# Order of the first loads, and the targets of routed rows, in a fused decoder layer

## The chip, the cores and the metric

The kernel runs on one core of one Trainium2 chip. The metric is the device time of one execution in microseconds (us). A core has TensorE (PE in the profile; its weight loads are PEld), VectorE (DVE), ScalarE (ACT), GpSimd (POOL) and SyncE (SP). Each engine works through its own queue of instructions in order. A DMA is issued by the queue of one engine, here SP or POOL, and moved by 16 DMA engines.

## The reference

A decoder layer in float32 on x of [4, 1024, 256], with a context of [4, 154, 256] and distances of [4, 1024, 154]:

```python
# self part: 16 heads of 16, queries modulated, beside a 4-head attention of the same tokens,
# and a 4-head attention over their mixture
mod = sigmoid(x @ cg_W + cg_b + (cons_vec @ am_W + am_b))
scores = (q @ k.T) / sqrt(16) * mod
ctx = 0.3 * softmax(scores) @ v + 0.7 * mha(x, x, ca)
ctx = 0.85 * ctx + 0.15 * mha(ctx, ctx, mc)
x = layernorm(x + ctx @ Wo + bo)
# cross part: 16 heads, bias from the distances
scores = (x @ Wq.T + bq) * 0.25 @ (c @ Wk.T + bk).T - log(distances + 1e-9) * abs(scaling)
x = layernorm(x + softmax(scores) @ (c @ Wv.T + bv) @ Wo.T + bo)
# feed-forward: the two best of 8 experts for each token, and a shared one
y = sum_e w[e] * (silu(x @ w_gate[e]) * (x @ w_up[e])) @ w_down[e]
out = layernorm(x + y + shared(x))
```

The meta weight 0.15 comes from (0.9 - 0.8) / 0.2 * 0.3.

## The kernel before

The work falls into a prologue, a loop over the four batches, the routing, the shared expert with the routed tiles, and a closing layernorm. Every tile is allocated from pools, and each engine's instructions stand in the order in which a scheduler at build time has put them; semaphores are placed where one engine's result is needed by another. DMAs of one kind (those of SP, those of POOL) take turns on eight completion semaphores, so that a DMA is issued only when the one eight places before it has landed.

**Prologue.** It loads the first batch (y0) and all attention weights and biases. `load_head_cols` loads a 256x256 weight through a staging tile, clears a tile of 128x1024 and copies each head's 16 columns into a field of 32 (L146, L148, on POOL). `load_head_bias` does the like with a bias in four small DMAs (L164, on POOL's queue); `load_cols` (L169) and `load_bcast` (L174) issue bias loads on POOL's queue too. `load_plain` (L138) issues weights on SP. The bias cgb of the modulation comes from four small matmuls (L212) on am and cons. The last loads of the prologue are the cross attention's weights and nds, the negated distance scaling. Then two DMAs on SP fill a DRAM tensor, `scratch` (9216 rows of 258 values): L260 writes zeros from `empty` into 256 of the 258 columns, L261 writes `rows` into the last two, of which the first is a row number of its own for each row, as the target of rows that no token fills.

**A batch's beginning**, the generator `begin(b)`. It transposes the tokens (L127, copied out by ACT at L130), fills v16 with ones on POOL (L761), projects mod, q and k for the first group of four heads (L288 with cgw, wq, wk; ACT at L392 and L408, POOL at L395, DVE at L401), and runs ahead with the first 12 steps of row maxima: a step is two row-tiled matmuls of q and k (L422) into a two-bank PSUM tile and one reduction on DVE (L429). Between the steps come the values v (L302 with wv, DVE at L310), after them the values of the second attention (L302 with cawin). Every eight steps the maxima are transposed (L343) and added to q (L346). For batches 1 to 3 this generator is spread over the cross part of the batch before; for batch 0 it is run through before the main loop of the batch. Ahead of it stand the loads of that batch's distances and context (L816, L818) on SP.

**The main loop** of a batch has 128 steps: maxima of step n+12, scores of step n (L460) into the three small PSUM banks and one more, exponentials on ACT (L471), and every fourth step the product with v (L480). At the steps 4, 8 and 12 of a group the next group is projected. The logarithm of the distances (L942 on ACT, with table loads of its own ahead of and behind it) and its product with nds (L943 on DVE) are written much later in the program, but have only the loads as inputs, and are put early in the queues by the scheduler.

**Routing and experts.** Gate probabilities give each token two experts, and from these a `place` in `scratch` for each of the two copies of a token. `tail` carries for each copy the row of `result` to which the expert's output goes (first of its two columns) and its weight. `send(b)` scatters tokens with their tails to `scratch` by indirect DMAs from POOL (L1127), beside the shared expert's matmuls (L1178, L1155). Then 72 tiles of 128 rows are fetched (L1198); `to` and `by` are taken from the two last columns (L1201, L1202 on POOL), the expert is applied (L1226, L1236, L1243, L1248), and the output is scattered to `result` by an indirect DMA over `to` (L1258).

Of the kernel before, what the change touches and what calls it, by code (L numbers as in the profile page):

```python
# [8 lines left out]
F32 = mybir.dt.float32  # L9
# [3 lines left out]
ALU = mybir.AluOpType  # L13
# [3 lines left out]
P = 128  # L17
B, S, H = 4, 1024, 256
# [4 lines left out]
NH, HD = 16, 16  # L23
# [10 lines left out]
RW = H + 2  # L34
TILES = 72
CAUSAL_W = 0.7
META_W = (0.9 - 0.8) / 0.2 * 0.3
# [3 lines left out]
def run(gen):  # L41
    for _ in gen:
        pass
# [3 lines left out]
def decoder_layer(ctx: ExitStack, tc: tile.TileContext, a, out):  # L47
    nc = tc.nc
# [25 lines left out]
    def load_y(b):  # L74
        ys.append(ypool.tile([P, NT, H], F32, tag="y", name=f"y{b}", bufs=2))
        nc.sync.dma_start(ys[b], xd[b])
# [12 lines left out]
    gw = const.tile([P, NC2, NE], F32, name="gw")  # L89
    dram = ctx.enter_context(tc.tile_pool(name="dram", bufs=1, space=bass.MemoryType.DRAM))  # L90

    scratch = dram.tile([TILES * P, RW], F32, name="scratch")
# [3 lines left out]
    def iota(dst, pattern, base, per_partition):  # L96
        nc.gpsimd.iota(
            dst,
            pattern=pattern,
            base=base,  # L100
            channel_multiplier=per_partition,
            allow_small_or_imprecise_dtypes=True,
        )
# [29 lines left out]
    with tc.tile_pool(name="wA", bufs=1) as wA, tc.tile_pool(name="work", bufs=2) as work:  # L133


        def load_plain(name, src, n):
            t = wA.tile([P, src.shape[0] // P, n], F32, tag=name, name=name)
            nc.sync.dma_start(t, src.rearrange("(c p) n -> p c n", p=P))  # L138
            return t

        def load_head_cols(name, src):

            st = work.tile([P, NC2, H], F32, tag="ex", name="stage", bufs=EXB)
            nc.sync.dma_start(st, src.rearrange("(c p) n -> p c n", p=P))
            t = wA.tile([P, NC2, NH, 32], F32, tag=name, name=name)
            nc.gpsimd.memset(t, 0.0)  # L146
            for c in range(NC2):
                nc.gpsimd.tensor_copy(  # L148
                    t[:, c, :, 0:HD], st[:, c, :].rearrange("p (h d) -> p h d", d=HD)
                )  # L150
            return t.rearrange("p c h w -> p c (h w)")

        def load_head_bias(name, src, extra):

            t = wA.tile([P, NG], F32, tag=name, name=name)
            if extra == 0.0:
                nc.vector.memset(t, 0.0)
            else:
                tmp = work.tile([P, NG], F32, tag="tmpb", name="tmpb")
                nc.vector.memset(tmp, extra)  # L160
                nc.vector.tensor_scalar(t, tmp, rowmx, None, ALU.mult)
            v = src.rearrange("(g j d) -> j d g", j=4, d=HD)
            for j in range(4):
                nc.gpsimd.dma_start(t[32 * j : 32 * j + HD, :], v[j])  # L164
            return t

        def load_cols(name, src):
            t = wA.tile([P, src.shape[0] // P], F32, tag=name, name=name)
            nc.gpsimd.dma_start(t, src.rearrange("(c p) -> p c", p=P))  # L169
            return t  # L170

        def load_bcast(name, src):
            t = wA.tile([P, H], F32, tag=name, name=name)
            nc.gpsimd.dma_start(t, src.unsqueeze(0).to_broadcast([P, H]))  # L174
            return t


# [7 lines left out]
            nc.gpsimd.memset(m, 0.0)  # L185
            mxcol.append(m)

        nc.sync.dma_start(gw, a["L0_ffn_gate_w"].rearrange("(c p) e -> p c e", p=P))
        wq = load_head_cols("wq", a["L0_attn_Wq"])
        bq = load_head_bias("bq", a["L0_attn_bq"], 0.0)  # L190

        cgs = work.tile([P, NC2, NH], F32, tag="cgs", name="cgs", bufs=1)
# [21 lines left out]
            )  # L214
        nc.vector.tensor_scalar(cgb, ps[:, 0:NG], 0.5, None, ALU.mult)

        wk = load_head_cols("wk", a["L0_attn_Wk"])
        bk = load_head_bias("bk", a["L0_attn_bk"], -1.0)
        wv = load_plain("wv", a["L0_attn_Wv"], H)
        bv = load_bcast("bv", a["L0_attn_bv"])  # L220
# [1 line left out]
        def load_mha(k, w_out):  # L222
            win = load_plain(k + "win", a[f"L0_attn_{k}_Win"], 3 * H)
            bin_ = a[f"L0_attn_{k}_bin"]
            mbq = load_cols(k + "bq", bin_[0:H])
            mbk = load_cols(k + "bk", bin_[H : 2 * H])
            mbv = load_bcast(k + "bv", bin_[2 * H : 3 * H])
            wout = load_plain(k + "wout", a[f"L0_attn_{k}_Wout"], H)
            bout = load_cols(k + "bout", a[f"L0_attn_{k}_bout"])
            nc.vector.tensor_scalar(bout, bout, w_out, None, ALU.mult)  # L230
            return win, mbq, mbk, mbv, wout, bout

        ca = load_mha("ca", CAUSAL_W)
        load_y(1)
        mc = load_mha("mc", META_W)
        wo = load_plain("wo", a["L0_attn_Wo"], H)
        bo = load_bcast("bo", a["L0_attn_bo"])
        xwq = load_head_cols("xwq", a["xWqT"])
        xbq = load_head_bias("xbq", a["L0_xattn_bq"], 0.0)
        xwk = load_head_cols("xwk", a["xWkT"])  # L240
        xbk = load_head_bias("xbk", a["L0_xattn_bk"], 0.0)
        xwv = load_plain("xwv", a["xWvT"], H)
        xbv = load_bcast("xbv", a["L0_xattn_bv"])
        xwo = load_plain("xwo", a["xWoT"], H)
        xbo = load_bcast("xbo", a["L0_xattn_bo"])

        nds = wA.tile([P, 1], F32, tag="nds", name="nds")
        nc.gpsimd.dma_start(nds, a["ds"].to_broadcast([P, 1]))
        nds2 = work.tile([P, 1], F32, tag="nds2", name="nds2", bufs=1)
        nc.vector.tensor_scalar(nds2, nds, -1.0, None, ALU.mult)  # L250
        nc.vector.tensor_tensor(nds, nds, nds2, ALU.min)


        empty = work.tile([P, H], F32, tag="avq", name="empty", bufs=3)
        nc.gpsimd.memset(empty, 0.0)
        rows = work.tile([P, TILES, 2], F32, tag="rb", name="rows", bufs=1)
        nc.gpsimd.memset(rows, 0.0)
        iota(rows[:, :, 0], [[P, TILES]], 2 * B * S, 1)
        sv = scratch.rearrange("(t p) w -> p t w", p=P)
        nc.sync.dma_start(sv[:, :, 0:H], empty.unsqueeze(1).to_broadcast([P, TILES, H]))  # L260
        nc.sync.dma_start(sv[:, :, H:RW], rows)  # L261


        def ex_tile(shape, name):
# [480 lines left out]
        def add_bias(y, bias):  # L745
            for t in range(NT):
                nc.gpsimd.tensor_tensor(y[:, t, :], y[:, t, :], bias, ALU.add)
# [5 lines left out]
        def begin(b):  # L753

            y = ys[b]
            xT = work.tile([P, NC2, S], F32, tag="xT", name="xT", bufs=1)
            for c in range(NC2):
                transpose_tokens(xT, y, c)
                yield
            v16 = work.tile([P, NT, VP], F32, tag="v16", name="v16", bufs=1)  # L760
            nc.gpsimd.memset(v16, 1.0)  # L761
            sa = Self(xT, v16, None)
            for step in (sa.project_mod, sa.project_q, sa.project_k):
                step(0)
                yield
            add_bias(y, bo)
            v64 = work.tile([P, NT, H], F32, tag="v64", name="v64", bufs=1)
            begun[b] = sa, xT, v64
            vals = values(xT, wv, 0, bv, v16, NH, HD, 1)
            for n in range(lead):  # L770
                sa.maxima(n)
                next(vals, None)
                sa.clock.step()
                yield
            yield from values(xT, ca[0], 2 * H, ca[3], v64, MH, MD, 0)

        def end(b, cx4):
# [28 lines left out]
            if b < B - 2:  # L806

                nc.sync.dma_start(kept[b].rearrange("(t p) d -> p t d", p=P), y)
                load_y(b + 2)

        behind = iter(())
        for b in range(B):
            y = ys[b]
# [3 lines left out]
            cn = work.tile([HK, 2, H], F32, tag="cn", name="cn", bufs=1)  # L817
            nc.sync.dma_start(cn, a["ctx_1024"][b].rearrange("(c p) d -> p c d", p=HK))  # L818

            if b == 0:  # L820
                run(begin(0))
            sa, xT, v64 = begun[b]
            sa.ctok = ctok = work.tile([P, NT, H], F32, tag="ctok", name="ctok", bufs=1)
            total = 16 * 8
# [177 lines left out]
    def rt(name, shape, dt=F32):  # L1002
        return xp.tile(shape, dt, tag=name, name=name)
# [9 lines left out]
    tail = rt("tail", [P, 2, NTT, 2])  # L1013
    ob = k1("ob", (P, 2, P))
    ones, before = ob[:, 0, :], ob[:, 1, :]
    iota(steps, [[P, NTT]], 0, 0)
    iota(tileno, [[1, TILES]], 0, 0)
    iota(tail[:, :, :, 0], [[B * S, 2], [P, NTT]], 0, 1)
    nc.gpsimd.memset(ones, 1.0)
    make_upper_triangular(nc, before, 1.0, diag=False)  # L1020

    red = rt("red", [P, NTT])
# [69 lines left out]
    for k in range(2):  # L1092
        mine = k1("mine")
        nc.vector.tensor_tensor(mine, hot[k], rank, ALU.mult)
        nc.vector.reduce_sum(red, mine, axis=AX.X)
        nc.vector.tensor_copy(place[:, k, :], red)


    owner = fw.tile([1, TILES, NE], F32, tag="hT", name="owner")
# [96 lines left out]
    def fetch(i):  # L1196
        xg = k1("xg", (P, RW))
        nc.sync.dma_start(xg, scratch[i * P : (i + 1) * P, :])  # L1198
        to = fw.tile([P, 1], U32, tag="to", name="to", bufs=5)
        by = fw.tile([P, 1], F32, tag="by", name="by", bufs=5)  # L1200
        nc.gpsimd.tensor_copy(to, xg[:, H : H + 1])  # L1201
        nc.gpsimd.tensor_copy(by, xg[:, H + 1 : H + 2])  # L1202
        ps = small()
        for c in range(NC2):
            nc.tensor.transpose(ps[:, c * P : (c + 1) * P], xg[:, c * P : (c + 1) * P], ident)
        xt = k1("xt", (P, NC2 * P))
        nc.scalar.copy(xt, ps[:, 0 : NC2 * P])
        xts[i] = xt, to, by
# [130 lines left out]
```

## Time and profile before

| | us |
|---|---|
| median of 3 runs | 3435.27 |
| lowest, highest | 3431.95, 3436.01 |
| the profiled execution's own time | 3433.82 |
| its span in the profile | 3432.0 |
| PE busy in the span | 3300.5 (96%) |
| DVE busy | 1725.3 (50%) |
| ACT busy | 1601.0 (47%) |
| POOL busy | 373.3 (11%) |

The profile is one execution. Times within it count from the start of the span. Its page shows the span in 40 slices of 85.8 us (a digit is a busy share in tenths; PEclk is the TensorE clock that was granted), the DMA queues, the chain of work that ended last, the costliest groups of instructions and the DMA issues. A line Lnnn is a line of the kernel. From the trace itself come the timeline, windows of chosen stretches, and the chain in order of time. An `x` behind a group counts instructions; a float32 matmul that is not a transpose is two of them.

### The profile page before, as it was taken

The numbers are of one execution on the slowest core, as the hardware profiler recorded it, in microseconds if no ns is written. First come the engines' busy times: TensorE is split into PE (matmuls) and PEld (weight loads), VectorE is DVE, ScalarE is ACT, GpSimd is POOL, SyncE is SP. The second block draws the span as 40 slices with busy tenths as digits, with TensorE's granted clock in tenths as the row PEclk, the third lists the DMA queues.
The fourth block names the chain that finished last, engine by engine and source line by source line (L and its number), as shares of the span: only waits on it lengthen the run. The fifth ranks groups of instructions, "written<-read, shape, count | busy, mean of one in ns | idle before, by whom it ended". The sixth has DMA issues, their size and how long they took to land.

```text
span 3432.0 us, 60936 instructions
## 1 busy us (share of the span) xinstructions
PE 3300.5 (96%) x25260; PEld 2085.6 (61%) x25260; DVE 1725.3 (50%) x3571; ACT 1601.0 (47%) x3130; POOL 373.3 (11%) x601
## 2 busy tenths in 40 slices
PE   7999999999999999999999999999999999999997
PEld 4555667565556675665566756555667665555554
DVE  3565555565655555656555556565556551122224
ACT  1555534375555453755554537555534731222223
POOL 4000000000000000000000000000000018222123
PEclk7999999999999999999999999999999999999999
DMA  9000000000000000000000000000000052111114
GB/s 204 1 2 1 1 1 1 3 21 14 1 1 1 1 1 3 21 13 2 1 1 1 1 3 9 1 2 1 1 1 1 1 203 82 47 42 44 44 44 157
DMA packets 75866, 84.13 MB, mean 25 GB/s; under 512 B 15136, under 2 KB 65928, under 8 KB 75592
## 3 DMA queue, kind: packets, MB, share of 16 engines
q1 hardware_dynamic: 68040, 61.53, 6.4%
q0 software_dynamic: 7552, 18.70, 1.6%
q8 instruction: 202, 3.31, 0.4%
q14 instruction: 72, 0.59, 0.1%
HBM read 46.52 MB, written 33.69 MB: 23 GB/s over the span
## 4 chain that ended last, share of the span: by engine, by line
PE 85%; DVE 9%; ACT 2%; issue 2%; POOL 1%; DMA 1%; SPq 0%; ACTq 0%; DVEq 0%; POOLq 0%
PE big L288 10%; PE big L422 8%; PE big L530 8%; PE one L566 7%; PE acc L584 7%; PE big L1226 7%; PE one L480 7%; DVE mxp L429 6%; PE one L460 4%; PE acc L1248 4%; PE one L697 3%; PE big L1178 3%; PE big L662 3%; PE one L302 2%; PE acc L716 2%
## 5 line engine op out<-in xcount | busy, mean ns | idle before, releaser
L429 DVE TENSOR_REDUCE mxp<-big 128x2 f32<-128x1024 f32 x512 | 610.3, 1218 | 305.5 <-PE acc L460 252.1
L422 PE MATMUL big<-k,q 31*128 31x512 f32 x2048 | 595.8, 644 | 30.2 <-DVE mxp L429 26.6
L471 ACT ACTIVATE ex<-one 128x512 f32<-128x512 f32 x696 | 391.3, 601 | 247.4 <-PE acc L460 182.9
L460 PE MATMUL one<-q,k 32*128 32x256 f32 x2784 | 501.9, 397 | 0.0
L269 DVE CUSTOM_DVE_ANT_0 prob<-big,zero_t 128x1024 f32<-128x1024 f32 x256 | 303.6, 1222 | 271.9 <-PE big L530 271.7
L460 PEld LDWEIGHTS one<-q,k 32*128 32x128 f32 x2784 | 326.8, 186 | 31.0 <-ACT ex L471 2.5
L549 ACT ACTIVATE prob<-prob,nmx 128x1024 f32<-128x1024 f32 x256 | 293.0, 1153 | 20.2 <-DVE nmx L269 19.7
L530 PE MATMUL big<-mk,mq 64*128 64x512 f32 x1024 | 284.4, 633 | 2.5 <-ACT ex L468 2.5
L422 PEld LDWEIGHTS big<-k,q 31*128 31x128 f32 x2048 | 180.1, 189 | 171.5 <-DVE mxp L429 93.6
L571 ACT COPY pt<-one 128x512 f32<-128x512 f32 x256 | 137.8, 588 | 311.7 <-PE one L566 311.7
L566 PEld LDWEIGHTS one<-ident,prob 128*128 128x128 f32 x2048 | 221.8, 142 | 98.1 <-issue 92.4
L1226 PE MATMUL big<-wall,xt 128*128 x576 | 272.5, 596 | 1.8 <-POOL by L1202 1.8
L460 PE MATMUL acc<-q,k 32*128 32x256 f32 x928 | 263.9, 404 | 0.0
L566 PE MATMUL one<-ident,prob 128*128 128x128 f32 x2048 | 257.6, 279 | 0.0
L480 PE MATMUL one<-ex,v 128*32 128x256 f32 x4096 | 248.4, 382 | 0.0
L1236 DVE TENSOR_TENSOR hidr<-big,slr 128x512 f32<-128x512 f32 x72 | 49.8, 691 | 332.7 <-ACT slr L1234 332.7
L682 ACT ACTIVATE xs<-xs,xmx 128x154 f32<-128x154 f32 x512 | 174.4, 414 | 69.6 <-DVE xmx L269 69.6
L480 PEld LDWEIGHTS one<-ex,v 128*32 128x32 f32 x4096 | 119.8, 110 | 122.1 <-ACT ex L471 35.8
L573 DVE COPY pt<-one 128x512 f32<-128x512 f32 x256 | 164.3, 683 | 10.9 <-PE one L566 10.9
L269 DVE CUSTOM_DVE_ANT_0 xs<-big,bias 128x154 f32<-128x154 f32 x512 | 132.0, 314 | 66.0 <-ACT avx L724 33.5
L530 PEld LDWEIGHTS big<-mk,mq 64*128 64x128 f32 x1024 | 99.6, 191 | 101.7 <-issue 79.4
L460 PEld LDWEIGHTS acc<-q,k 32*128 32x128 f32 x928 | 155.4, 186 | 0.0
(266 smaller groups left out, 4715.2 us busy)
## 6 DMA issues: line engine op xcount, KB each, us to landing
xg<-scratch SPq DMA_DIRECT2D x72, 129.0 KB, 2.0
scratch<-empty SPq DMA_DIRECT2D x1, 9216.0 KB
r<-result SPq DMA_DIRECT2D x8, 1024.0 KB, 11.2
y<-in_x_dram SPq DMA_DIRECT2D x4, 1024.0 KB, 5.3
wall<-in_L_ffn_w_gate_dram SPq DMA_DIRECT2D x8, 512.0 KB, 10.3
wall<-in_L_ffn_w_up_dram SPq DMA_DIRECT2D x8, 512.0 KB, 10.8
wall<-in_L_ffn_w_down_dram SPq DMA_DIRECT2D x8, 512.0 KB, 11.6
bias<-in_fside_BxSxS_dram SPq DMA_DIRECT2D x4, 616.0 KB, 4.5
```

Source lines behind the costliest of these rows:

```text
L269: nc.vector.tensor_tensor_reduce(out=out, in0=ps, in1=bias, scale=-1.0, scalar=3.0e38, op0=ALU.add, op1=ALU.min, accum_out=low,)
L288: nc.tensor.matmul(ps[:, tb, :], w[:, c, lo : lo + P], xT[:, c, tb * 512 : (tb + 1) * 512], start=(c == 0), stop=(c == NC2 - 1),)
L422: nc.tensor.matmul(ps[:, jj, :], st["q"][r : r + MR, tok : tok + P], st["k"][r : r + MR, kb * 512 : (kb + 1) * 512], start=True, stop=True,)
L429: nc.vector.reduce_max(mxp[:, t, kb, 2 * pair : 2 * pair + 2], ps, axis=AX.X)
L460: nc.tensor.matmul(scs[jj][:, i * QW : (i + 1) * QW], st["k"][r : r + MR + 1, kc * P : (kc + 1) * P], st["q"][r : r + MR + 1, part * QW : ...
L471: nc.scalar.activation(ex[:, jj, :], scs[jj], AF.Exp, scale=1.0 / HD**0.5)
L480: nc.tensor.matmul(av[32 * j : 32 * j + 32, 0:QW], self.v[:, kc, h * VW : h * VW + 32], exs[kc // 2, j // 2][:, j % 2, i : i + QW], start= ...
L530: nc.tensor.matmul(pss[i][:, kb, :], q[r : r + MD, t * P : (t + 1) * P], k[r : r + MD, kb * 512 : (kb + 1) * 512], start=True, stop=True,)
L549: nc.scalar.activation(p, p, AF.Exp, bias=nmx[:, i : i + 1], scale=-1.0, accum_out=sm[:, t % 4, i : i + 1],)
L566: nc.tensor.transpose(ps[:, kc * P : (kc + 1) * P], probs[u][i][:, at : at + P], ident)
L584: nc.tensor.matmul(av[64 * i : 64 * i + 64, (t % 4) * P : (t % 4 + 1) * P], v[:, kc, h * MD : (h + 1) * MD], flipped[u][i][:, kc, :], star ...
L1226: nc.tensor.matmul(ps[:, g, :], xt[:, c * P : (c + 1) * P], wall[:, bass.ds(off + (g * NC2 + c) * D, D)], start=(c == 0), stop=(c == NC2 - 1),
```

## The change

It has four parts. All small loads that stood on POOL's queue are issued by SP. The clearing and copying of wq and wk are done on DVE, those of xwq and xwk stay on POOL. The loads which the first batch's beginning does not need (the second batch's y, the gate, mc, Wo, the cross attention's weights and nds, the fill of scratch) stand in the program behind `run(begin(0))`, which is itself now ahead of the load of the distances. And the fill of scratch is one DMA of zeros over all 258 columns: `tail` holds a token's target less 8192 and the row that it is placed in, and a new tile, `own`, holds 8192 and the row's number (the row's own target) and is added when the tile is fetched, on DVE instead of POOL.

```diff
-        def load_head_cols(name, src):
+        def load_head_cols(name, src, eng):
...
-            nc.gpsimd.memset(t, 0.0)
+            eng.memset(t, 0.0)
             for c in range(NC2):
-                nc.gpsimd.tensor_copy(
+                eng.tensor_copy(
...
-                nc.gpsimd.dma_start(t[32 * j : 32 * j + HD, :], v[j])
+                nc.sync.dma_start(t[32 * j : 32 * j + HD, :], v[j])
...
-            nc.gpsimd.dma_start(t, src.rearrange("(c p) -> p c", p=P))
+            nc.sync.dma_start(t, src.rearrange("(c p) -> p c", p=P))
...
-            nc.gpsimd.dma_start(t, src.unsqueeze(0).to_broadcast([P, H]))
+            nc.sync.dma_start(t, src.unsqueeze(0).to_broadcast([P, H]))
...
-        wq = load_head_cols("wq", a["L0_attn_Wq"])
+        wq = load_head_cols("wq", a["L0_attn_Wq"], nc.vector)
...
         ca = load_mha("ca", CAUSAL_W)
-        load_y(1)
-        mc = load_mha("mc", META_W)
-        wo = load_plain("wo", a["L0_attn_Wo"], H)
         bo = load_bcast("bo", a["L0_attn_bo"])
-        xwq = load_head_cols("xwq", a["xWqT"])
...
-        empty = work.tile([P, H], F32, tag="avq", name="empty", bufs=3)
-        nc.gpsimd.memset(empty, 0.0)
-        rows = work.tile([P, TILES, 2], F32, tag="rb", name="rows", bufs=1)
-        nc.gpsimd.memset(rows, 0.0)
-        iota(rows[:, :, 0], [[P, TILES]], 2 * B * S, 1)
-        sv = scratch.rearrange("(t p) w -> p t w", p=P)
-        nc.sync.dma_start(sv[:, :, 0:H], empty.unsqueeze(1).to_broadcast([P, TILES, H]))
-        nc.sync.dma_start(sv[:, :, H:RW], rows)
...
+        run(begin(0))
...
+        load_y(1)
+        nc.sync.dma_start(gw, a["L0_ffn_gate_w"].rearrange("(c p) e -> p c e", p=P))
+        mc = load_mha("mc", META_W)
+        wo = load_plain("wo", a["L0_attn_Wo"], H)
+        xwq = load_head_cols("xwq", a["xWqT"], nc.gpsimd)
...
+        empty = work.tile([P, RW], F32, tag="rb", name="empty", bufs=1)
+        nc.gpsimd.memset(empty, 0.0)
+        nc.sync.dma_start(
+            scratch.rearrange("(t p) w -> p t w", p=P),
+            empty.unsqueeze(1).to_broadcast([P, TILES, RW]),
+        )
...
             nc.sync.dma_start(cn, a["ctx_1024"][b].rearrange("(c p) d -> p c d", p=HK))
-            if b == 0:
-                run(begin(0))
...
+    own = rt("own", [P, TILES])
+    iota(own, [[P, TILES]], 2 * B * S, 1)
...
         nc.vector.tensor_copy(place[:, k, :], red)
+        nc.vector.scalar_tensor_tensor(
+            tail[:, k, :, 0], tail[:, k, :, 0], -2.0 * B * S, red, ALU.add, ALU.subtract
+        )
...
-        nc.gpsimd.tensor_copy(to, xg[:, H : H + 1])
+        nc.vector.tensor_tensor(to, xg[:, H : H + 1], own[:, i : i + 1], ALU.add)
```

More of the change, by code (lines that the diff above doesn't have):

```diff
@@ L186, in decoder_layer @@
             mxcol.append(m)
-        nc.sync.dma_start(gw, a["L0_ffn_gate_w"].rearrange("(c p) e -> p c e", p=P))
-        wq = load_head_cols("wq", a["L0_attn_Wq"])
+        wq = load_head_cols("wq", a["L0_attn_Wq"], nc.vector)
         bq = load_head_bias("bq", a["L0_attn_bq"], 0.0)
@@ L215, in decoder_layer @@
         nc.vector.tensor_scalar(cgb, ps[:, 0:NG], 0.5, None, ALU.mult)
-        wk = load_head_cols("wk", a["L0_attn_Wk"])
+        wk = load_head_cols("wk", a["L0_attn_Wk"], nc.vector)
         bk = load_head_bias("bk", a["L0_attn_bk"], -1.0)
@@ L233, in decoder_layer @@
         ca = load_mha("ca", CAUSAL_W)
-        load_y(1)
-        mc = load_mha("mc", META_W)
-        wo = load_plain("wo", a["L0_attn_Wo"], H)
         bo = load_bcast("bo", a["L0_attn_bo"])
-        xwq = load_head_cols("xwq", a["xWqT"])
[L239 to L251, printed above, removed]
-        empty = work.tile([P, H], F32, tag="avq", name="empty", bufs=3)
-        nc.gpsimd.memset(empty, 0.0)
-        rows = work.tile([P, TILES, 2], F32, tag="rb", name="rows", bufs=1)
-        nc.gpsimd.memset(rows, 0.0)
-        iota(rows[:, :, 0], [[P, TILES]], 2 * B * S, 1)
-        sv = scratch.rearrange("(t p) w -> p t w", p=P)
-        nc.sync.dma_start(sv[:, :, 0:H], empty.unsqueeze(1).to_broadcast([P, TILES, H]))
-        nc.sync.dma_start(sv[:, :, H:RW], rows)
         def ex_tile(shape, name):
@@ L809, in end @@
                 load_y(b + 2)
+        run(begin(0))
[4 more added lines that the diff above has]
+        xwq = load_head_cols("xwq", a["xWqT"], nc.gpsimd)
+        xbq = load_head_bias("xbq", a["L0_xattn_bq"], 0.0)
+        xwk = load_head_cols("xwk", a["xWkT"], nc.gpsimd)
+        xbk = load_head_bias("xbk", a["L0_xattn_bk"], 0.0)
+        xwv = load_plain("xwv", a["xWvT"], H)
+        xbv = load_bcast("xbv", a["L0_xattn_bv"])
+        xwo = load_plain("xwo", a["xWoT"], H)
+        xbo = load_bcast("xbo", a["L0_xattn_bo"])
+        nds = wA.tile([P, 1], F32, tag="nds", name="nds")
+        nc.sync.dma_start(nds, a["ds"].to_broadcast([P, 1]))
+        nds2 = work.tile([P, 1], F32, tag="nds2", name="nds2", bufs=1)
+        nc.vector.tensor_scalar(nds2, nds, -1.0, None, ALU.mult)
+        nc.vector.tensor_tensor(nds, nds, nds2, ALU.min)
+        empty = work.tile([P, RW], F32, tag="rb", name="empty", bufs=1)
[4 more added lines that the diff above has]
+        )
         behind = iter(())
```

## The prediction

> **What bounds the kernel now.** I read the 40 slices first: TensorE is the bound nearly everywhere, except in the first slice.
>
> ```profile
> PE   7999999999999999999999999999999999999997
> PEclk7999999999999999999999999999999999999999
> DMA  9000000000000000000000000000000052111114
> ```
>
> Slice one (86 us) alone has a TensorE that is neither full nor at full clock, under a busy DMA. Next the table of windows for that slice (columns: window, length, PE, PEld, DVE, ACT, POOL busy, then granted clock, DMA share, GB/s):
>
> ```profile
> 24.00:27.00 3.00, 2.89 (x9) 1.33 (x7) 0.82 (x2) 0.00 (x0) 3.00 (x6) 1.00 1.05 273
> 27.00:32.00 5.00, 0.00 (x0) 0.00 (x0) 0.00 (x0) 3.61 (x3) 5.00 (x11) 0.99 0.30 58
> 32.00:36.00 4.00, 0.00 (x0) 0.00 (x0) 2.45 (x5) 0.00 (x0) 3.91 (x5) 0.50 0.96 307
> 36.00:69.00 33.00, 30.85 (x71) 11.73 (x71) 17.62 (x22) 0.00 (x0) 4.90 (x8) 0.50 1.22 252
> 69.00:72.00 3.00, 3.00 (x9) 2.46 (x8) 1.65 (x2) 0.00 (x0) 0.00 (x0) 0.50 1.86 6
> 72.00:76.00 4.00, 4.00 (x18) 3.44 (x18) 1.70 (x4) 0.00 (x0) 0.00 (x0) 0.90 0.88 5
> ```
>
> PE stands still from 27 to 36 while POOL is full; the clock halves at 32 and comes back only at 73. The loss is 9 us of waiting and some 41 us at half rate. What ends the wait is in the chain of work that ended last:
>
> ```profile
> 14.99 5.96 DMA cabq<-in_L_attn_ca_bin_dram
> ...
> 26.81 0.74 POOL xwk L148 x2
> 27.55 1.46 POOL xbk L164 x3
> ...
> 30.09 3.31 DMA nds<-in_ds_dram
> ...
> 35.63 0.42 DVE v L310
> 36.09 2.08 PE one L302 x4
> ```
>
> The chain runs through POOL's queue of small loads: v16's fill and mod (L761, L395) stand behind every bias load, and on DVE the first q and v (L401, L310) stand behind nds. Last, the timeline, for what the zeros of the scratch do to a DMA behind them on SP, and for when the main loop first needs ACT:
>
> ```profile
> 33.25 26.62 SPq L261 DMA_DIRECT2D scratch<-rows  x1
> 84.13 1.08 ACT L471 ACTIVATE ex<-one 128x512 f32<-128x512 f32 x2 [0.23 <-PE one L460]
> 87.55 0.38 PE L343 MATMUL one<-ident,mxcol 128*128 128x128 f32 x2
> 87.86 1.93 PE L480 MATMUL one<-ex,v 128*32 128x256 f32 x32
> ```
>
> The small DMA behind the zeros took 26.62 us to issue, and the issue table gives it 45.0 us to land.
>
> **What the Trainium skill says.** "DMA: Bandwidth & Descriptors", section "Queues, rings and completion order": each DMA engine takes one issuing engine's descriptors in ring order. The trace agrees: scratch<-rows landed only at 78, after zeros that moved until 67. The same page, "Issuing engines are not separate DMA queues": moving loads from POOL to SP saves only sequencer time; here that time is the point, as a POOL issue holds POOL for 0.5 to 0.75 us. "TensorE: Matmul & The Clock Gate", Part 1: TensorE falls to half rate after an idle window of about 3.4 us and recovers after a busy one. The fall agrees (idle from 26.9, half at 32); the recovery doesn't follow busy time alone: PE was 30.85 of 33 us busy at half rate, and it came back only after the first full window of 128x128 L302 matmuls (from 69). I count the narrow 31-row L422 as too little activity.
>
> **The change, part by part.**
>
> *POOL and the first q.* Ahead of v16's fill POOL loses four memsets (0.94 to 0.97), eight copies (0.37 each) and 29 DMA issues. The issues go to SP, the memsets and copies of wq and wk to DVE (idle then), those of xwq and xwk behind v16's fill on POOL, where the memsets end near 11 and the copies come after mod. DVE memsets and copies of these shapes are not in the trace before; bounded by POOL's 0.94 and DVE's own 0.42 for a 128x256 copy, all is over by 14 us, beside the transposes: nothing. In the new instruction streams nds, mcbout and the bias multiply stand behind the first maxima. So q and k follow the projections. am_b, cg_b and cons become 9th to 11th on SP; from the ninth DMA on each waits for the one eight before, the ninth for y (6.3 in the timeline), so cons lands near 9.3 and the four L212 matmuls come at 9.6 instead of 8.68; eleven transposes now stand before them instead of five, so cgw's projection starts near 13, as before. Three projections of 3.6 to 4.5 us end at 24.6, k on ACT 1.1 later: first L422 at 26 instead of 38.1.
>
> *The beginning's second half.* Before it took 38.1 to 78.0: alternating L422 and L302 groups of 2.01 and 2.00 us each at half clock. PE's gap is now under 2 us, so I take full clock: six steps at 2.15 (half of 4.01 and something for latencies; DVE needs 1.22+0.42), 12.9; two first steps at DVE's pace, 2.4; four reduces at 1.35 and a row fold, 6.1; 32 L302 at 0.24 (six took 1.46), 7.8. Sum 29.2: the main loop starts at 55, 23 us sooner.
>
> *What is late next: bias.* The streams put 48 DMAs ahead of it on SP: after 6.3 some 40 more at 0.6 us each (L138 issues took 0.4 to 1.3) bring the zeros at 31 (28 to 35), by chance as before (30.97). They moved at 290 to 300 GB/s from 32 to 67; with 1032-byte rows 34.5 us. bias (0.63 MB, 2 us, and 1 to landing) comes behind them: 31+34.5+3 = 68.5, between 63 and 75. cn follows, needed only in the cross stage. On ACT the Ln on bias (1.32) and two table loads (1.28 each) now stand after the first six exponentials, which end at 82.8-23 = 59.8. ACT then waits for bias. Behind it on ACT: the exponentials of steps 3 and 4, and on DVE the bias multiply, then reduces. PE runs on to L343 (64.5), where no small PSUM bank is free. ACT must do Ln, a load and three exponentials (1.32+1.28+1.7): L480 starts at 68.5+4.3 = 72.8 instead of 87.86, a gain of 15.1. The second table load was already paid before Ln. Note that the end of this stall doesn't depend on how fast the beginning gets there, up to 9 us: it takes back 8 of the 23.
>
> *Clock after the stall.* An idle of 8 us halves the clock again; L480 and L288 are dense, so one or two windows of 3.4 us at half rate: 1.7 to 3.4 lost, I take 2.6.
>
> *Routing.* Two DVE operations of 128x32 (0.18 to 0.29 for such shapes) and one iota (0.22) stand ahead of the sends; POOL's sends end at 2920.2, a us before PE's shared part, which hides them but for a tail: 0.3 at most. In the routed loop `to` moves from POOL (0.19) to DVE (0.15 by nds): DVE idles 4.5 us ahead of each L1236, and xg is loaded well ahead: nothing; if its DMA were late, PE's L1205 would wait for it anyway. rows, its iota and its 72 KB in 8-byte pieces go: nothing waited for them.
>
> **Sum.** -15.1 + 2.6 + 0.3 = -12.2 us on the profiled execution's 3433.82 (span 3432.0, 1.8 around it): 3421.6. That execution is 1.4 below the median 3435.27, so the median becomes 3423.
>
> **Rivals.**
> *bias is not held up* (the zeros' descriptors let it pass, or zeros issue early): gain 23 less 1.3 (Ln and loads 3.9 on an ACT with 2.6 idle there) and 0.3: 3414. Against: the 45.0 us of scratch<-rows. Chance 0.18.
> *SP becomes the bound*: 48 waits on eight lanes at nearly 0.8 us put the zeros at 38, bias at 75.5, L480 at 79.8: -8.1+2.6+0.3 = -5.2, 3430; with 36 or later up to no gain. For: issues that rose to 1.3 us near 13 us. Chance 0.14 for a gain under 7.
> *Slower*: one place, the zeros. If a 1032-byte row goes in two packets, or as a costlier write, bias comes later than 80.7 and the sum turns: that is from about 47 us of zeros, 81 ns a packet on 16 engines against 50 to 69 in the trace. With an 8-byte packet's mean of 31 added to 62: 53.6 us, bias at 88, L480 at 92: +4.4+2.6+0.3 = 3443. Against: reads of xg ran as whole 1032-byte packets. Chance 0.06.
> That the early loads do not get shorter at all is excluded by the streams; a clock that stays half in the beginning would end it at 66, still hidden by the stall.
>
> **How the numbers follow.** The likeliest case (bias at 63 to 75, gain 6 to 18) has 0.62, of which 0.60 is beyond 0.2% (6.9 us, about what a measurement of this kernel can tell from no change). With the first rival faster is 0.78; same 0.15; slower 0.07, the third rival and a stray clock. The range goes from 3410, the first rival's 3414 with one cold window less, to 3433, the second rival's near end, and leaves out some 0.12.
>
> **What would show it.** Right: PE without a hole between 25 and 36, first L422 near 26, clock 1.00 to about 60; then an ACT wait ahead of L942 released by the DMA of bias, DVE's L943 behind it, PE idle some 8 us before L343, half clock for 3 to 7 us after. Wrong: bias landing before 60 (first rival), zeros issued after 36 (second) or taking over 45 us (third), PE cold from 26 on, or a change in the routed loop's pace of 6 us a tile.

## The result and the profile after

| | before | after |
|---|---|---|
| median, us | 3435.64 (4 runs) | 3460.19 (4 runs) |
| lowest, highest | 3431.95, 3436.79 | 3458.6, 3467.14 |
| span of the profiled execution | 3432.0 | 3456.8 |

The ratio is 1.0081, 95% interval 1.0067 to 1.0095: **slower by 25 us**, where 12 us less were predicted, and above the top of the range. New line numbers stand 28 below the old ones in the attention (L394 was L422, L432 was L460, L443 was L471, L452 was L480, L315 was L343), and six above them in the expert part (L1184 was L1178, L1193 was L1187, L1169 was L1163, L1207 was L1201).

First the 40 slices of the changed kernel.

```profile
PE   7999999999999999999999999999999995999997
PEclk9999999999999999999999999999999997999999
```

The first slice got its clock back (9 instead of 7). But slice 34, from 2852 to 2938 us, has a PE at 5 tenths with a clock at 7, and there the kernel before had nines. Both traces hold the same 25260 matmuls, so the start of the k-th one can be compared, counted in each from the start of its span. The changed kernel is 9.2 us ahead at 100 us and 12.5 ahead at 2865. At 2940 it is 31.7 behind, at 2957 25.5 behind, and it stays so through the routed loop, whose pace is unchanged. The prologue brought three quarters of what was predicted for it (9.2 of 12.5 us), then the shared expert's stretch lost 44.2 us and gave 6.2 back.

The shared expert works through three blocks of tokens. In each, DVE multiplies the two halves of the hidden layer (`hid`, L1193) and later adds the expert's output to the tokens (`res`, L1169, four adds a block). The timeline of DVE in that stretch (start, length, engine, line, operation; in brackets the idle time before it and what ended it):

```profile
2851.89 0.69 DVE L1193 TENSOR_TENSOR hid<-big,sl 128x512 f32<-128x512 f32 x1 [2.74 <-ACT sl L1192]
2854.71 0.69 DVE L1169 TENSOR_TENSOR res<-one,y0again 128x512 f32<-128x512 f32 x1 [2.13 <-PE one L1161]
2912.81 0.16 DVE L1207 TENSOR_TENSOR to<-xg,own 128x1 uint32<-128x1 f32 x1 [57.41 <-DMA xg<-scratch]
2912.89 1.88 DVE L1169 TENSOR_TENSOR res<-one,y0again 128x512 f32<-128x512 f32 x3
2914.69 1.28 DVE L1193 TENSOR_TENSOR hid<-big,sl 128x512 f32<-128x512 f32 x2
```

The scheduler put the first `to` between the first and the second of four res adds of the second shared block. It waited 57.41 us, and the three res adds behind it, ready long before, ran at once when it was through. The Trainium skill's page "PSUM — Partial Sum Buffer", section "Engine vs sequencer instructions", says that VectorE's queue is strict FIFO; the trace agrees with these 57.41 us. What TensorE did meanwhile:

```profile
2915.42 23.58 PE L1184 MATMUL big<-x2T,shw 128*128 128x512 f32 x48 [41.22 <-DVE hid L1193]
```

It ran on until 2874.2, then had no free PSUM tile: the hid products that were to read the full ones stood behind the res adds. It came back after 41.22 us at half clock (48 matmuls took 23.58 us, where 64 of the block before took 27.79), which makes the 41 us 44. The chain of work that ended last, in order of time, shows what the wait hung on:

```profile
2906.83 0.98 POOL scratch L1133
2908.12 2.58 DMA scratch<-st,place
2910.76 2.02 DMA xg<-scratch
2912.97 1.80 DVE res L1169 x3
2915.42 23.58 PE big L1184 x48
```

A tile of `scratch` may be fetched only when the last send has landed. So `to`, on an engine that the shared expert needs, tied the shared expert to the end of POOL's sends. Before, `to` stood on POOL itself, behind the last send, where nothing of the shared expert is queued:

```profile
2923.99 0.19 POOL L1201 CAST to<-xg 128x1 uint32<-128x1 f32 x1 [3.80 <-DMA xg<-scratch]
```

Of the 6.2 us given back 4.8 are the routed part's own start: before, PE waited 3.0 us for xg and 1.8 for `by` there, and now both had long been done. Most of the rest is the half-rate spell that followed these waits: the first four L1226 took 3.65 us before, 1.98 now.

Then the prologue, the timelines of SP, ACT and PE.

```profile
32.31 0.38 SPq L808 DMA_DIRECT2D scratch<-empty  x1
32.73 30.29 SPq L818 DMA_DIRECT2D bias<-in_fside_BxSxS_dram  x1
...
72.27 1.32 ACT L942 ACTIVATE bias<-bias,tiny_t 128x1232 f32<-128x1232 f32 x1 [13.12 <-DMA bias<-in_fside_BxSxS_dram]
...
76.53 3.64 PE L452 MATMUL one<-ex,v 128*32 128x256 f32 x32 [0.29 <-ACT ex L443]
```

As the prediction had it, bias is behind the zeros: its issue took 30.29 us, ACT stood 13.12 us for it, and L452 starts at 76.53 instead of 87.86. The logarithm is needed only in the cross part; like `to` it waits at a place in the queue where the next stage's work, here the exponentials, stands behind it. The table of windows, for the stretch shown of before (columns as there):

```profile
40.00:48.00 8.00, 7.66 (x32) 3.81 (x32) 7.02 (x10) 0.00 (x0) 0.00 (x0) 1.00 1.09 260
...
64.00:72.00 8.00, 0.00 (x0) 0.00 (x0) 0.00 (x0) 0.00 (x0) 0.00 (x0) 0.71 0.87 219
72.00:80.00 8.00, 4.16 (x34) 1.68 (x34) 2.42 (x3) 5.67 (x7) 1.05 (x1) 0.50 0.00 0
```

Full clock in the beginning, then a stretch in which no engine works while the DMA moves zeros, then half clock. PE itself stood 12.76 us, from 62.79 to 75.55.

### The profile page after: what moved, and what is told of

The parts are those of the page before. It is cut to its first block, busy times and chain, and to the rows that moved or that the text cites. A ratio compares the mean times of both kernels' runs of the same rounds, so it can differ in the third digit from the quotient of the medians.

```text
span 3456.8 us, 61047 instructions
## 1 busy us (share of the span) xinstructions
PE 3285.9 (95%) x25260; PEld 2077.5 (60%) x25260; DVE 1730.0 (50%) x3651; ACT 1601.0 (46%) x3130; POOL 346.2 (10%) x493
## 4 chain that ended last, share of the span: by engine, by line
PE 80%; DVE 9%; DMA 3%; ACT 3%; issue 3%; POOL 2%; SPq 0%; DVEq 0%; ACTq 0%; POOLq 0%
PE big L260 10%; PE big L502 8%; PE one L538 7%; PE big L394 7%; PE acc L556 7%; PE big L1232 7%; PE one L452 7%; DVE mxp L401 6%; PE one L432 4%; PE acc L1254 4%; PE one L669 3%; PE big L634 2%; PE acc L688 2%; PE big L602 2%; PE one L274 1%
## 5 line engine op out<-in xcount | busy, mean ns | idle before, releaser
L394 PE MATMUL big<-k,q 31*128 31x512 f32 x2048 | 587.7, 633 | 29.2 <-DVE mxp L401 25.6
L432 PE MATMUL one<-q,k 32*128 32x256 f32 x2784 | 502.7, 397 | 0.0
L443 ACT ACTIVATE ex<-one 128x512 f32<-128x512 f32 x696 | 391.2, 600 | 229.7 <-PE acc L432 185.2
L432 PEld LDWEIGHTS one<-q,k 32*128 32x128 f32 x2784 | 327.3, 186 | 31.2 <-ACT ex L443 2.5
L394 PEld LDWEIGHTS big<-k,q 31*128 31x128 f32 x2048 | 177.8, 186 | 166.4 <-DVE mxp L401 86.3
L432 PE MATMUL acc<-q,k 32*128 32x256 f32 x928 | 264.3, 404 | 0.0
L452 PE MATMUL one<-ex,v 128*32 128x256 f32 x4096 | 250.1, 384 | 0.3 <-ACT ex L443 0.3
L452 PEld LDWEIGHTS one<-ex,v 128*32 128x32 f32 x4096 | 120.0, 110 | 123.2 <-ACT ex L443 36.5
L1184 PE MATMUL big<-x2T,shw 128*128 128x512 f32 x256 | 116.2, 614 | 46.1 <-DVE hid L1193 43.8
## 6 DMA issues: line engine op xcount, KB each, us to landing
r<-result SPq DMA_DIRECT2D x8, 1024.0 KB, 11.8
```

The source lines that it names most:

```text
L394: nc.tensor.matmul(ps[:, jj, :], st["q"][r : r + MR, tok : tok + P], st["k"][r : r + MR, kb * 512 : (kb + 1) * 512], start=True, stop=True,)
L432: nc.tensor.matmul(scs[jj][:, i * QW : (i + 1) * QW], st["k"][r : r + MR + 1, kc * P : (kc + 1) * P], st["q"][r : r + MR + 1, part * QW : ...
L443: nc.scalar.activation(ex[:, jj, :], scs[jj], AF.Exp, scale=1.0 / HD**0.5)
L452: nc.tensor.matmul(av[32 * j : 32 * j + 32, 0:QW], self.v[:, kc, h * VW : h * VW + 32], exs[kc // 2, j // 2][:, j % 2, i : i + QW], start= ...
```

## The experiments

Theory 1: the place of the first `to` in VectorE's queue makes the loss. Theory 2: the routing itself became slower. For the prologue: bias waits only because of what stands ahead of it on SP. The ratio is that to the kernel before, measured beside each on the same chip (there its medians were 3433.4 to 3435.6); L452 is the first product with the exponentials, L480 or L478 where the loads are not moved.

| kernel | us | 95% interval of the ratio | first L452, us |
|---|---|---|---|
| before | 3435.6 | | 87.86 |
| after | 3460.2 | 1.0067 to 1.0095 | 76.53 |
| after, `to` on GpSimd | 3423.4 | 0.9962 to 0.9992 | 74.53 |
| after, `to` held back on VectorE | 3427.3 | 0.9967 to 0.9998 | 74.91 |
| before, routing half only | 3467.8 | 1.0081 to 1.0111 | 87.92 |
| after, routing half undone | 3437.5 | 1.0008 to 1.0025 | 87.54 |
| after, zeros behind bias | 3447.4 | 1.0023 to 1.0047 | 63.45 |
| `to` on GpSimd, zeros behind bias | 3417.2 | 0.9938 to 0.9964 | 63.35 |
| `to` held back, zeros behind bias | 3415.9 | 0.9935 to 0.9962 | 63.98 |
| before, order of loads only | 3430.7 | 0.9983 to 1.0000 | 83.12 |
| before, queues only | 3443.6 | 1.0023 to 1.0049 | 94.88 |

Single executions of one kernel differ by up to some 20 us here, the longer ones with a lower mean clock (with `to` on GpSimd 3418.8 us at 0.981 and 3439.95 at 0.974). The traces have half-rate stretches at varying places of the main loop: in the profile of the kernel with `to` held back such a stretch from 734 to 748 took 6 of its 10.7 us of lead. Differences of medians below some 6 us are therefore read from the traces.

**`to` back on GpSimd.**

```diff
-        nc.vector.tensor_tensor(to, xg[:, H : H + 1], own[:, i : i + 1], ALU.add)
+        raw = fw.tile([P, 1], F32, tag="raw", name="raw", bufs=5)
+        nc.gpsimd.tensor_tensor(raw, xg[:, H : H + 1], own[:, i : i + 1], ALU.add)
+        nc.gpsimd.tensor_copy(to, raw)
```

> The changed kernel, but the add that makes `to` goes back to GpSimd (an add into a float tile and a copy to integers), as the copy stood before; everything else of the change stays. Theory 1 (head of VectorE's queue): in the changed kernel the first `to` stands in VectorE's queue between the res adds of the shared expert, waits 57.4 us for the scatter and the gather, and costs a stall of 44.2 us less 6.2 regained, 38. On GpSimd it stands behind the last send, where nothing else is queued. Then the time is 3460.2 - 38 = 3422, the shared expert's matmuls follow each other without the 41 us hole, and the prologue's gain of 11.6 remains. Theory 2 (the routing itself is slower: relative targets, rows in one piece, order on SyncE's queue): the hole stays or reappears ahead of the first routed tile, about 3460.

Measured 3423.4, 36.8 less than after. The waits of PE from 2850 to 2960 (engine, line, what it waited for: us in total, times, longest) have no L1184 above 0.2 us left:

```profile
PE one L1213 <- DMA xg<-scratch: 3.4, 1, 3.4
PE big L1234 <- POOL by L1210: 1.5, 1, 1.5
PE big L1184 <- ACT x2T L130: 0.2, 1, 0.2
```

The waits for xg and `by` are back, as before the change, and the prologue's gain remains (12.6 us ahead of before at 2865). Theory 1 holds.

**`to` held back on VectorE.** Is it the place or the engine?

```diff
+    late = rt("late", [P, TILES])
+    nc.vector.scalar_tensor_tensor(
+        late, res[1][:, NT - 1, 0:TILES], 0.0, own, ALU.mult, ALU.add
+    )
...
-        nc.vector.tensor_tensor(to, xg[:, H : H + 1], own[:, i : i + 1], ALU.add)
+        nc.vector.tensor_tensor(to, xg[:, H : H + 1], late[:, i : i + 1], ALU.add)
```

> The changed kernel with `to` still an add on VectorE, but its second operand is a copy of `own` made from the last result of the third shared block (own plus zero times res), so that no `to` can stand in VectorE's queue ahead of the shared expert's adds. Theory 1 (it is the place in the queue, not the engine): as with `to` on GpSimd, 3423, no wait of VectorE ahead of the first `to` beyond a few us. Rival (VectorE is the wrong engine for it: the add from float to integers is dear, or each `to` delays the routed adds): some of the 38 us stays, from 3430 up to 3460, spread over the routed loop.

Measured 3427.3. The group of all 72 adds (busy us, mean ns, idle before and its releaser):

```profile
L1207 DVE TENSOR_TENSOR to<-xg,late 128x1 uint32<-128x1 f32 x72 | 10.8, 150 | 3.7 <-DMA xg<-scratch 2.6 <-DMA result<-yo,to 1.1
```

In the changed kernel the same 72 adds had 58.5 us of idle before them. VectorE is no worse an engine for it: the 0.15 us of the prediction was right, the queue place was not looked at. The 3.9 us to the 3423.4 with GpSimd are within the scatter of executions.

**The routing half alone**: the kernel before with `own`, the subtraction in `tail`, one DMA of zeros and the add on VectorE.

> The kernel before with the routing half of the change alone: targets stored relative to the place, one DMA of zeros, `to` as an add on VectorE; all loads stay where they were. Theory 1: the hole is independent of the loads' order, so the time is 3435.6 + 38 = 3473, plus or minus 4 (the second small DMA to the scratch is gone, which may bring bias, at 78 before, up to 10 us sooner; nothing waits for it there). Theory 2 (the hole comes from the moved loads together with the routing): about 3436.

Measured 3467.8, 34 above before on that chip (3434.0), and a little under the 3473 plus or minus 4. The waits from 2790 to 2970:

```profile
DVE to L1205 <- DMA xg<-scratch: 56.3, 1, 56.3
...
PE big L1182 <- DVE hid L1191: 40.1, 1, 40.1
```

The same stop without any moved load; the traces give 41.8 lost and 6.2 given back, 35.6. A remark in that expectation is mistaken: 78 was the landing of `rows`; bias was ready before 28 us in the kernel before, as it is here.

**The loads alone**: the changed kernel with the routing half undone (the 72 KB of `rows` in 8-byte pieces are back, `to` is a copy on GpSimd).

> The changed kernel with the routing half undone: absolute targets in the scratch by a second DMA of 8-byte pieces, `to` copied on GpSimd; the loads stand behind the first batch's beginning. Theory 1: no hole in the shared expert. Its gain is then the prologue's alone, and bias stands on SyncE behind both the zeros and the 8-byte pieces, which took 10 us more before (67 to 77): bias lands near 80 instead of 72 and the matmuls that need it start near 84 instead of 76.5, a gain of 0 to 4: 3432 to 3436. Rival (the 8-byte pieces cost little when they run beside the zeros): bias as in the changed kernel, about 3424. Theory 2 in the form that the moved loads make the hole: about 3460.

Measured 3437.5: no stop in the shared part, and no gain either; it is 3.5 us slower than before on that chip. SP's and ACT's timelines:

```profile
31.91 30.28 SPq L813 DMA_DIRECT2D scratch<-rows  x1
62.24 16.70 SPq L820 DMA_DIRECT2D bias<-in_fside_BxSxS_dram  x1
...
83.28 1.32 ACT L944 ACTIVATE bias<-bias,tiny_t 128x1232 f32<-128x1232 f32 x1 [23.95 <-DMA bias<-in_fside_BxSxS_dram]
```

Behind zeros and rows bias comes 11 us later than behind zeros alone, and L452 at 87.54 stands where it stood before. The start of the main loop moved by 24.7 us and the time did not: all of it was turned into a wait for bias. So the routing half of the change is what makes the loads half worth something: 11 us in the prologue, by the rows that go. It then spends 38 on `to`.

**Zeros behind bias**, on the kernel with `to` on GpSimd.

```diff
-        empty = work.tile([P, RW], F32, tag="rb", name="empty", bufs=1)
-        nc.gpsimd.memset(empty, 0.0)
-        nc.sync.dma_start(
-            scratch.rearrange("(t p) w -> p t w", p=P),
-            empty.unsqueeze(1).to_broadcast([P, TILES, RW]),
-        )
         behind = iter(())
         for b in range(B):
...
             nc.sync.dma_start(cn, a["ctx_1024"][b].rearrange("(c p) d -> p c d", p=HK))
+            if b == 0:
+                empty = work.tile([P, RW], F32, tag="rb", name="empty", bufs=1)
+                nc.gpsimd.memset(empty, 0.0)
+                nc.sync.dma_start(
+                    scratch.rearrange("(t p) w -> p t w", p=P),
+                    empty.unsqueeze(1).to_broadcast([P, TILES, RW]),
+                )
```

> As the kernel with `to` on GpSimd, and the DMA of zeros is issued after the first batch's bias and cn on SyncE instead of ahead of them. Theory of the prologue: bias waits only because 4.2 MB of zeros stand before it in the same queue; behind nothing it lands near 41, ScalarE's Ln and exponentials run as soon as their inputs are there, the first matmuls on exponentials start at 63 to 64 instead of 76.5, and no cold window follows (2.6): 11 to 13 us less than with the zeros ahead, about 3410. Rival (the zeros' traffic slows whatever comes then, cn or y of the next batch, or the beginning of the loop waits for something else): about 3422, as without the move.

Measured 3417.2, between the two figures expected. (The 4.2 MB in that expectation is a slip: the zeros are 9288 KB.) The timelines of SP, ACT and PE:

```profile
31.63 0.43 SPq L811 DMA_DIRECT2D bias<-in_fside_BxSxS_dram  x1
...
32.74 0.38 SPq L818 DMA_DIRECT2D scratch<-empty  x1
...
38.54 1.32 ACT L943 ACTIVATE bias<-bias,tiny_t 128x1232 f32<-128x1232 f32 x1 [11.28 <-DMA bias<-in_fside_BxSxS_dram]
...
63.35 1.93 PE L452 MATMUL one<-ex,v 128*32 128x256 f32 x32
```

And the page's row of the zeros (KB, us from issue to landing):

```profile
scratch<-empty SPq DMA_DIRECT2D x1, 9288.0 KB, 37.5
```

bias's issue takes 0.43 us instead of the 26 to 30 with the zeros ahead, its logarithm runs at 38.54, before the first exponentials, and L452 follows at 63.4 as expected. By the traces the main loop is 24.5 us ahead of before from there, 12.4 more than with the zeros ahead; the medians show 6.2 of it.

**Zeros behind bias with `to` as the change has it.**

> The changed kernel, with `to` where the change put it, and only the DMA of zeros issued after the first batch's bias and cn on SyncE. If the two causes are independent, the stop ahead of the first `to` stays (its end is set by GpSimd's sends, which follow the main loop), and the beginning gains what it gained with `to` on GpSimd, where the first matmuls on exponentials came 12.4 us sooner in the traces (6 us in the medians): 3460.2 less 6 to 12, 3448 to 3454, still slower than before. If an earlier main loop only makes the wait for the sends longer, nothing is gained: 3460.

Measured 3447.4, 12.8 below after and just under the 3448 to 3454. The stop is whole, with a wait of 54.6 us ahead of `to`; within the scatter the two causes are independent.

**Both taken away, `to` on VectorE.**

> Both causes taken away with `to` on VectorE: the late copy of `own` as in the experiment with `to` held back, and the zeros behind the first batch's bias and cn. Independent causes: 3427.3 less 6 to 12, 3415 to 3421, the same as with `to` on GpSimd and the zeros behind (3417). If VectorE is dearer for `to` than GpSimd: above 3421.

Measured 3415.9, 11.3 below the same kernel with the zeros ahead, and level with 3417.2. The three pairs of kernels with and without the zeros ahead thus differ by 6.2, 12.8 and 11.3 us in their medians. These two are the best versions found, **0.5% below before**.

**The order of the loads alone.** The blocks of loads moved as in the change; every small load, fill and copy stays on GpSimd.

> The kernel before with the later loads moved behind the first batch's beginning, all small loads still issued by GpSimd, the head weights' fills and copies still there, routing as before. The prediction laid the early first q to GpSimd having 29 DMA issues, four fills and eight copies fewer ahead of the values' fill. Theory A (the order is what counts): 15 of the issues and half of the fills and copies leave GpSimd's way, 13 us of it, so the first maxima start near 26 as in the changed kernel. In this kernel's queues bias stands ahead of the zeros on SyncE; its multiply on VectorE stands among the first maxima behind nds, which GpSimd issues only near 36, so a stop of some 10 us comes there: main loop near 60, first matmuls on exponentials near 72, 3420 plus or minus 6. Theory B (the issuing queue is what counts): the first maxima start at 31 or later, and the gain is under 5: above 3429.

Measured 3430.7. The chain in order of time:

```profile
27.29 2.77 POOL y L719 x4
30.06 0.67 POOL mcbq L169
...
32.01 2.96 DMA mcbout<-in_L_attn_mc_bout_dram
...
35.00 0.96 DVE mcbout L229
```

Neither theory had this. The time falls on theory B's side (above 3429), but the first maxima start at 25.5, as theory A says, and the next stop comes from mcbout, not nds. Its issue stands on GpSimd behind eight adds of 0.69 us, and its scaling on VectorE among the first maxima. After it the clock is at half until the window from 64 to 72, and 4.7 us are left of the gain. It is again an instruction at the head of VectorE's queue that waits for a DMA issued late.

**The queues alone.** The loads in the old order, issued by SP, wq and wk on VectorE.

> The kernel before with the loads in the old order, but the small loads issued by SyncE and the fills and copies of the first two head weights on VectorE; routing as before. Theory A (order): on VectorE the first maxima stand behind nds, which is near the end of SyncE's 40-odd issues, 30 us plus 3 to land: first maxima near 33 instead of 36 to 38. Theory B (queue): near 26. In both cases bias stands behind the zeros and the 8-byte rows, as in the kernel with the loads alone (landing near 80), and ScalarE's logarithm on it ahead of the first exponentials, so that the first matmuls on exponentials start at 84 to 88: 3432 to 3437, little or no gain.

Measured 3443.6, slower than before (3433.4 on that chip), and above the 3432 to 3437 of both theories. The first maxima start at 35.8, for another reason than nds: q waited for GpSimd's mod, which stood behind adds that waited 14.33 us for the load of bo, late in SP's long row. ACT then stood 48.89 us until bias, behind zeros and rows, had landed; the main loop's first scores were there from 68 on:

```profile
82.17 1.32 ACT L942 ACTIVATE bias<-bias,tiny_t 128x1232 f32<-128x1232 f32 x1 [48.89 <-DMA bias<-in_fside_BxSxS_dram]
```

The Trainium skill's "DMA: Bandwidth & Descriptors", section "Issuing engines are not separate DMA queues", leaves only sequencer time to be saved by the queue; with the order unchanged this run has its first maxima 2.3 us sooner than before and its first L480 7 us later. So the order alone brings the first maxima forward. The main loop starts at 78.0 before, at 73.2 with the order alone, at 67.2 with the queues alone and at 53.1 with both. What the order alone would give without the late mcbout was not tested.

## Why the prediction was wrong

**The failing step is "Routing".** It gave the moved `to` a cost of nothing, since DVE idles 4.5 us ahead of each L1236 and xg is loaded well ahead; "if its DMA were late, PE's L1205 would wait for it anyway". That holds inside the routed loop, where the runs agree: PE's distance to before stays at 25.5 us from 2957 to 3327 us. But the first `to` does not stand in the loop. In DVE's queue its turn came 57 us before its input was there, ahead of 3 res adds and all hid products of the next block, and these, not L1205, wait for it. The other half of the same step, that the sends end a us before PE's shared part, "which hides them", was a cover only as long as nothing in the shared part waited for the sends. The term +0.3 measured +44.2 - 6.2 = +38.0. No rival had it; the slower one looked to the zeros, and its sign, zeros of over 45 us, did not come (37.5).

**The other terms held**, with errors that fit the range:

- The first q: 26 predicted, 25.81 measured. The main loop: 55 predicted, 53.05 measured, with steps of 2.12 us where 2.15 was taken.
- bias: 68.5 predicted, 72.3 measured. The zeros were issued at 32.3 instead of 31, and they take 37.5 us from issue to landing (measured in the kernel with the zeros behind bias) where 34.5 was counted; bias's logarithm began 2.5 us after that, where 3 was counted.
- From bias to the first L452 4.26 us passed, 4.3 predicted. The gain there is 11.3 instead of 15.1. PE ran out of work 1.7 us sooner than predicted and bias came 3.8 later, so PE stood 12.76 us where some 8 were predicted.
- The clock after the stall: 2.6 predicted; the lead fell from 11.3 to 9.2, so 2.1.
- Together -9.2 at 100 us, where -12.5 was predicted. It became -11.8 between 333 and 355 us, where the kernel before had a half-rate stretch that this one has not; that nears the sum of -12.2 by luck, not by the terms.

With 38.0 in place of 0.3 the sum is 25.5 above the profiled execution; the spans differ by 24.8; that they agree so well owes something to the same luck. The rivals of the prologue: SP did not become the bound (zeros at 32.3, not 38), and bias was held up; the first rival's figure of 3414 is what the kernel gives once both waits are really gone (3415.9 and 3417.2).

## What to carry to other kernels

An operation moved to another engine is costed at the place where the new engine's queue has it, not where the program writes it: find what it waits for, and count every instruction that is queued behind it until that comes, first of all for the first of a series, which a scheduler can hoist out of its loop. Even on an engine that idles half its time, 0.15 us of work can stand at a place in the queue where it costs 38 us. A big DMA belongs behind the small ones that the next stage needs; a start that is brought forward gains only up to the next late load.

## What the runs showed of the hardware

The clock of TensorE depended on where it came from, for the same mixture of instructions. The alternating groups of 31-row maxima matmuls and values kept it at full rate in the changed kernel, where they began at full rate (1.00 from 24 to 56 us, PE busy 7.3 to 8 of each 8 us). They did not bring it back where they began at half: it stayed at 0.50 from 36 to 69 before, and from 36 to 64 in the kernel with only the order changed, where PE was busy 7.45 to 8 of each 8 us from 40 on. A step took 4.01 us at half rate, 2.12 at full rate. "TensorE: Matmul & The Clock Gate", Part 1, lets a busy window of 3.4 us restore it; here some 30 us of such work did not. It came back while the 32 dense values matmuls of 128 rows (L302 or L274 with cawin) ran: 3.5 to 3.8 us after their start in these two kernels, 5.4 us after it with the queues alone.

Nor did a fall need a long stop. In the kernel with only the order changed the clock fell at 30.3, when PE's stop of 6.21 us had lasted 0.2 us; ahead of the stop lay 2.2 us of work and a gap of 1.31 us. In the kernel with `to` held back it fell at 45.1 for 3.4 us, behind a stretch of almost only maxima matmuls with one gap of 0.34 us. What in these matmuls counts for the clock is not shown.

A DMA issued on SP right behind the 9216 or 9288 KB of zeros was held in the issue itself for 26 to 30 us, in seven kernels, and what followed it in SP's queue with it (cn in the changed kernel, issued only at 63.06). Ahead of the large one bias's issue took 0.43 to 1.25 us, in three kernels.
